# Two graph layers on one core: 0/1 matrices turned by bf16 products, a PSUM bank for the nodes alone, and a later first row-by-row tile

## The chip, the core and the metric

The kernel runs on one core of a Trainium2 chip. The metric is device time in microseconds: 3799.89 us, the median of three runs (3799.22 to 3804.44). One further execution was profiled; the views quoted below come from it.

A core has five engines, each working through its own instructions in order: PE (TensorE: matrix products, written to PSUM), DVE (VectorE), ACT (ScalarE), POOL (GpSimd; here it issues almost only indirect DMAs, which gather rows of a table by an index column) and SP (SyncE; here it issues plain DMAs). They wait for each other by semaphores. PSUM holds 8 banks of 128 partitions by 512 float32.

## The reference

Two message-passing layers over 6250 nodes and 200000 edges, which are sorted by their target `dst`, each behind a layer norm and a relu:

```
h = relu(layernorm(x))
z = h @ W                                   # 8 heads of 16
el, er = z.attn_l, z.attn_r                 # per head
e = leaky_relu(el[src] + er[dst], 0.2)
a = exp(e - segment_max(e, dst)[dst])
x = x + segment_sum(z[src] * a, dst) / segment_sum(a, dst) + bias
h = relu(layernorm(x))
s, v = h parts @ W_up                       # 32 scalars, 32 vectors of 3
w = silu(silu(edge_attr_8 @ A1 + b1) @ A2 + b2) @ A3
m = segment_sum(products of s[src], v[src], edge_attr_4 and w, dst) / 10
x = x + m @ W_out
```

## The kernel before

**Tiles and blocks.** The edges are cut into 1563 tiles of 128, the tiles into 98 blocks of `KB` = 16 (the last has 11 tiles). For a tile the kernel needs the 128 rows of a node table that `src` names: table `t0` (136 floats a row: z and el) in the first layer, `t1` (128 floats) in the second. They come to a buffer `z` of a block in four ways:

- `gather` (L839): one indirect DMA on POOL for one tile. It is the usual way: 2972 of them in all.
- `rows_by_row` (L1142): for the last tile of each block in the list `by_row` (L1109), SP issues 128 plain DMAs, one per row, into a tile `r`; `filled` (L1167) has ACT copy it into `z`. `rows_by_row` is a generator that hands back after 4 DMAs, and `rows_until(rows, block)` (L1162) draws from it until a count that follows the block number. `by_row` is 3, 6, ..., 93 in both layers.
- Dense blocks (first layer: 21 to 93 where not in `by_row`): tile 14 of the block is computed on PE as a product of 0/1 matrices with the whole table, which lies in SBUF in three bf16 parts (`t0s`). `asked(k)` (L1255) loads three tiles of the table into `zr` by SP, `split(k)` (L1270) has DVE cut them into the parts.
- The rows of the first block and of 7 tiles of block 1 (`KX = KB + 7`, L806) are gathered from `x` itself before `t0` exists, and `v["rows_of"]` (L1129) computes z and el for them on the spot.

There are five buffers for `z` besides `z_first`, used in turn. The gathers of block g+5 overwrite those of block g, and each waits for the product that last read its tile.

**The loop of the first layer.** After a prologue (layer norm and `t0` for all nodes, the check that the edges are sorted evenly), one turn g of a loop (L1570) works on several blocks at once: `logits(c)` and `maxima(c)` for block g, the attention weights and `sums` of block g-1, and `masks_of`, `turned`, `er_of` and `er_sum` for block g+1. The order of PE, DVE, ACT and SP is the written order; POOL's is too, since gathers alone stand on it. The first turns place this on SP: `rows_until(rows, g + 0.5)`, node outputs, `asked(g - 2)`, `node_rows`, `rows_until(rows, g + 1)`; and `split(g - 3)` at the end of the turn on DVE.

- `one_hot` (L1174): DVE compares `iota_p` with the local target of each edge; the result `s` is a 0/1 matrix of 128 edges by 128 nodes in float32, four tiles at a time. It is the stationary operand of `sums` (L1420).
- `turned` (L1332): PE transposes `s`, a float32 transpose per tile, into bank `p_d`; ACT copies it to bf16 `d` (L1339). `er_of` (L1341) multiplies `d` by the node values er, and `er_sum` (L1352) adds the three bf16 parts.
- `masks_of` (L1323): one product into bank `p_m` and a copy to `mk`, 385 columns: 128 for same target as the edge before, a separating column that is always -1e30, 128 for same target as the first edge of the next tile, 128 for the last of the tile before.
- `node_x` to `node_out` (L1436 to L1491): in every second turn, two blocks have completed 64 nodes each; the new x, its layer norm and the rows of `t1` are computed: `node_t` transposes into `p_n` (L1467), ACT makes `h_t` (L1469), `node_s` multiplies by W_up into `p_n` (L1474), ACT writes `sv` (L1479), and SP stores it to `t1` and to `t1z`, a copy of `t1` whose last three tiles are zero.

The bank `p_n` (L1247) is shared: the node products, `iota_p` (read by each `one_hot`) and `er_p` (written by each `er_sum`, read by the next `logits`) lie in it.

**Between the layers.** The last turn is g = 95; the blocks behind it follow in straight code (L1661 on). The first 24 gathers of the second layer (`early`, L1667) read `t1z`, which is complete when the last node tile but three is stored; the gathers after them read `t1` and wait for its last store. The second layer starts the same way, with `rows_by_row` for `t1` and its own unit loop (`tensor_weights`, `messages`, `sums1`).

Of the kernel before, what the change touches and what calls it, by code (L numbers as in the profile page):

```python
# [741 lines left out]
def tile_even_edges(  # L742
# [31 lines left out]
    TG = -(-TU // P)  # L774
    NB = -(-TU // KB)
    KT = [min(KB, TU - b * KB) for b in range(NB)]
    MC = 3 * P + 1
    assert NB % 2 == 0 and NB > 4 and KT[-1] > 3 and NX == NB // 2 + 1
    dram = ctx.enter_context(tc.tile_pool(name="fdram", bufs=1, space=DRAM))
    keep = ctx.enter_context(tc.tile_pool(name="keep", bufs=1))  # L780
# [22 lines left out]
    src_col = keep.tile([P, TU], I32, name="fsrc")  # L803
    z_first = keep.tile([P, KB, ZW], F32, name="fz_first")
    ok_i = keep.tile([1, 1], I32, name="fok")
    KX = KB + 7  # L806
    z_second = keep.tile([P, KB, ZW], F32, name="fz_second")
    other = keep.tile([P, KB, ZW], F32, name="fz_other")
    flat = other.rearrange("p k f -> p (k f)")
# [201 lines left out]
def even_edges(tc, v):  # L1011
# [8 lines left out]
    with ExitStack() as ctx:  # L1020
# [41 lines left out]
        with tc.tile_pool(name="fbuild", bufs=1) as build:  # L1062
# [21 lines left out]
            nc.vector.memset(eq[:, :, P : P + 1], 0.0)  # L1084
            nc.vector.tensor_tensor(eq[:, :, :P], e_i, q_i, OP.is_equal)
            nc.vector.memset(eq[:, :, 0:1], 0.0)
            nc.vector.tensor_tensor(eq[:, :, P + 1 : 2 * P + 1], e_i,
                                    nxt_i.to_broadcast([P, TG, P]), OP.is_equal)
            nc.vector.tensor_tensor(eq[:, :, 2 * P + 1 :], e_i,
                                    q_i[:, :, 0:1].to_broadcast([P, TG, P]), OP.is_equal)  # L1090
            for g in range(TG):
                nc.scalar.activation(masks[:, g, :], eq[:, g, :], AF.Copy, bias=-BIG, scale=BIG)
# [13 lines left out]

            by_row = [b for b in range(3, NB - 2) if b % 3 == 0]  # L1109
            at = [const.tile([P, P], I32, name=f"fat{i}") for i in range(2)]  # L1110
            with tc.tile_pool(name="fat_ps", bufs=1, space=PSUM) as at_ps, \
                    tc.tile_pool(name="fat_c", bufs=1) as at_c:
# [29 lines left out]
        def rows_by_row(layer, table, width):  # L1142

            flat = table.rearrange("r f -> (r f)").bitcast(mybir.dt.uint8)
            size = 4 * width
            for b in by_row:
                to = row_pool.tile([P, width], F32, name="r")
                rows_by_row.tiles[layer, b] = to
                for e in range(P):
                    if e % 32 == 0:  # L1150
                        _, offs = nc.values_load_multi_w_load_instructions(
                            at[layer][b : b + 1, e : e + 32], engines=[mybir.EngineType.SP],
                            min_val=0, max_val=(NX * P - W0 - 1) * size,
                            skip_runtime_bounds_check_because="a row of the table")
                    nc.sync.dma_start(to[e : e + 1, :].bitcast(mybir.dt.uint8),
                                      flat[ds(offs[e % 32], size)].unsqueeze(0))
                    if e % 4 == 3:
                        yield
# [2 lines left out]

        def rows_until(rows, block):  # L1162

            while rows_until.n < (block + 3) * P / 12 and next(rows, 0) is None:
                rows_until.n += 1

        def filled(layer, b, z, width):  # L1167
            if b in by_row:
                nc.scalar.copy(z[:, KB - 1, :width], rows_by_row.tiles.pop((layer, b)))

        def one_hot(t, m, iota, pool=s_pool):
# [29 lines left out]
        dense = {b for b in range(-(-NX // TS) + 4, NB - 4) if b not in by_row}  # L1201
        dense1 = set(range(10, NB - 4, 4))

        ranges = []
# [34 lines left out]
        with tc.manual_schedule(engines=in_order), \  # L1239
# [83 lines left out]
            def masks_of(c):  # L1323
                o, kr = c["o"], c["kt"] * H
                g, j = divmod(c["b"], P // KB)
                p_m = l0_ps.tile([P, 512], F32, name="p_m")
                nc.tensor.matmul(p_m[:kr, :MC], rsel[:, j, o * H : o * H + kr], masks[:, g, :],  # L1327
                                 start=True, stop=True)
                mk = c["mk"] = l0.tile([P, MC], F32, name="mk", bufs=4)
                nc.scalar.copy(mk[:kr], p_m[:kr, :MC])  # L1330

            def turned(c, q):  # L1332
                if 4 * q < c["kt"]:
                    m = min(4, c["kt"] - 4 * q)
                    p_d = l0_ps.tile([P, 4, P], F32, name="p_d")
                    for k in range(m):
                        nc.tensor.transpose(p_d[:, k, :], c["s"][q][:, k, :], ident)  # L1337
                    d = c["d", q] = l0.tile([P, 4, P], BF, name="d", bufs=4)
                    nc.scalar.copy(d[:, :m], p_d[:, :m])  # L1339

            def er_of(c, q):  # L1341
                if 4 * q < c["kt"]:
                    b = c["b"]
                    er_w = (er3o if b % 2 else er3)[:, b // 2, :, :].rearrange("p s h -> p (s h)")
                    if q == 0:
                        c["p_er"] = l0_ps.tile([P, KB, 3, H], F32, name="p_er")
                    for k in range(min(4, c["kt"] - 4 * q)):
                        nc.tensor.matmul(c["p_er"][:, 4 * q + k].rearrange("p s h -> p (s h)"),
                                         c["d", q][:, k, :], er_w, start=True, stop=True)

            def er_sum(c, aside=False):
                kt = c["kt"]  # L1352
                er = c["er"] = l0.tile([P, KB, H], F32, name="er") if aside else er_p
                nc.vector.tensor_reduce(er[:, :kt], c["p_er"][:, :kt].rearrange("p t s h -> p t h s"),
                                        AX.X, OP.add)

            def logits(c, bank="pe"):
# [9 lines left out]
            def maxima(c):  # L1367

                kr, mk, pe = c["kt"] * H, c["mk"], c["pe"]
                m0, m1 = pe[:kr, P : 2 * P], pe[:kr, 3 * P :]  # L1370
                nc.vector.tensor_tensor_scan(m0, mk[:kr, :P], pe[:kr, :P], 0.0, OP.add, OP.max)
                nc.vector.tensor_tensor_scan(m1[:, ::-1], mk[:kr, P:0:-1], m0[:, ::-1], 0.0,
                                             OP.add, OP.max)
                mx = c["mx"] = l0.tile([P, 2], F32, name="mx", bufs=4)
                nc.scalar.copy(mx[:kr], m1[:, :: P - 1])
# [18 lines left out]
            def weights(c):  # L1394

                kr, pe, mk, ud = c["kt"] * H, c["pe"], c["mk"], c["ud"]
                m1, m2 = pe[:kr, 3 * P :], pe[:kr, P : 2 * P]
                nc.vector.scalar_tensor_tensor(m2, mk[:kr, P + 1 : 2 * P + 1], ud[:kr, 0:1],
                                               m1, op0=OP.add, op1=OP.max)
                a = l0.tile([P, P], F32, name="a")  # L1400
                nc.vector.scalar_tensor_tensor(a[:kr], mk[:kr, 2 * P + 1 :], ud[:kr, 1:2],
                                               m2, op0=OP.add, op1=OP.max)
                nc.vector.tensor_sub(a[:kr], pe[:kr, :P], a[:kr])
                nc.scalar.activation(a[:kr], a[:kr], AF.Exp)
# [111 lines left out]
            def take_rows(g):  # L1516
                if g == 1:
                    cs[1]["z"] = gather(buffer(), t0, range(KX, 2 * KB), ZW, KX - KB)
                elif 0 < g < NG:
                    c = cs[g]  # L1520
                    t = c["b"] * KB + c["o"]
                    c["z"] = gathered(t0, [k for k in range(t, t + c["kt"])
                                           if not (c["b"] in by_row and k % KB == KB - 1)
                                           and not (c["b"] in dense and k % KB == KD)], ZW)

            def bank_of(c, bank="p_u"):
                if c["o"] == 0:
                    bank_of.now = l0_ps.tile([P, 512], F32, name=bank)
                c["p_u"] = bank_of.now

            def ended(c, st):
# [161 lines left out]
            neighbours(c1, c2, None)  # L1693
            weighted(c3, 0)
            sums(c4, 8)
            bank_of(c3, "p_m")
            sums(c3, 0)
            weights(c2)
            weights(c1)
# [28 lines left out]
        with tc.manual_schedule(engines=in_order), \  # L1728
# [209 lines left out]
            def take_rows(b):  # L1938
# [2 lines left out]
                                         max(NE - b * KB, 0))  # L1941
                elif b < NB:
                    blk[b]["z"] = gathered(t1, [k for k in range(b * KB, b * KB + KT[b])
                                                if not (b in by_row and k % KB == KB - 1)
                                                and not (b in dense1 and k % KB == KD)], P)

            rows, rows_until.n, late, x_of = rows_by_row(1, t1, P), 0, [], {}
# [13 lines left out]
            for i, u in enumerate(us):  # L1961
# [196 lines left out]
```

## Time and profile before

| | |
|---|---|
| time, median of three runs | 3799.89 us |
| time of the profiled execution | 3804.17 us |
| span of the profiled execution | 3802.3 us |
| mean granted TensorE clock | 0.915 of full speed |
| PE busy | 3119.3 us (82%) |
| DVE busy | 2560.8 us (67%) |
| ACT busy | 1412.3 us (37%) |
| POOL busy | 2836.8 us (75%), 3005 instructions |
| gathers on POOL (L839) | 944 ns each |
| row DMAs on SP | 3968 in each layer |

The first layer's loop lies at about 82 to 1896 us, the second layer from about 1929 us on. A busy share is an average: an engine that issues DMAs spends time between two of them that isn't counted as busy. A line of the timeline gives the start, the duration, the engine, the source line, the operation with its tiles and shapes, and how many instructions follow each other; in brackets stands how long the engine had been idle before and what ended that. A line of the waits gives the waiting instruction, what it waited for, the sum in us, how often, and the longest.

### The profile page before, as it was taken

What the parts mean: (1) busy time and instruction counts of PE and PEld (TensorE: products, weight loads), DVE (VectorE), ACT (ScalarE), POOL (GpSimd) and SP (SyncE); (2) the same over time, 40 slices, a digit from 0 to 9 for tenths busy, and PEclk for the clock granted to TensorE, in tenths of its full rate; (3) what the DMA queues carried; (4) which work ended last, traced back from release to release, by engine and by line L of the source; (5) the groups of instructions that cost most, each with busy time, mean ns of one, the idle gap of its engine ahead of it and who ended that gap; (6) DMA issues with size and microseconds to landing.
All of it is one profiled execution on the core that took longest, in us unless ns stands there. A gap on an engine that the chain in (4) does not pass through costs nothing. (4 is left out here: it accounts for less than half of the span.)

```text
span 3802.3 us, 72404 instructions
## 1 busy us (share of the span) xinstructions
PE 3119.3 (82%) x18514; PEld 2471.7 (65%) x18514; DVE 2560.8 (67%) x6137; ACT 1412.3 (37%) x3637; POOL 2836.8 (75%) x3005
## 2 busy tenths in 40 slices
PE   5466687888887787787787898999999899999997
PEld 4466566666666666666666677677677677777775
DVE  7366666666666656666556777777777777777776
ACT  4233333333333333333324444444444444444443
POOL 7677777777777777777677777777777777777776
PEclk7666698988998998999789999999999999999999
DMA  6233323322222223222223222222222222222222
GB/s 163 56 78 78 78 67 68 69 68 68 68 68 70 68 68 68 68 68 69 60 68 93 75 64 63 64 63 64 64 64 63 64 64 63 64 64 64 64 68 52
DMA packets 213547, 264.35 MB, mean 70 GB/s; under 512 B 77936, under 2 KB 164560, under 8 KB 213120
## 3 DMA queue, kind: packets, MB, share of 16 engines
q0 software_dynamic: 95840, 202.46, 22.5%
q1 hardware_dynamic: 116848, 57.10, 5.5%
q8 instruction: 148, 2.42, 0.3%
q14 instruction: 279, 2.29, 0.2%
q10 hardware_dynamic: 432, 0.09, 0.0%
HBM read 237.94 MB, written 21.14 MB: 68 GB/s over the span
## 5 line engine op out<-in xcount | busy, mean ns | idle before, releaser
L839 POOL DMA_INDIRECT fz<-ft,fsrc x1764 | 1665.9, 944 | 558.4 <-issue 323.8
L1817 PE MATMUL p_u<-mj,s 128*128 128x256 f32 x3126 | 761.6, 387 | 87.6 <-DVE mj L1809 86.6
L1817 PEld LDWEIGHTS p_u<-mj,s 128*128 128x128 f32 x3126 | 579.5, 191 | 214.7 <-DVE mj L1809 139.4
L839 POOL DMA_INDIRECT fz_other<-ft,fsrc x594 | 561.0, 944 | 181.2 <-issue 106.7
L839 POOL DMA_INDIRECT fz_second<-ft,fsrc x590 | 559.7, 949 | 182.8 <-issue 108.3
L1784 ACT ACTIVATE p_w<-p_w,yb 128x64 f32<-128x64 f32 x1563 | 450.4, 288 | 117.1 <-PE p_w L1780 73.3
L1306 PE MATMUL p_x<-t0s,fz_first 128*128 128x408 bf16 (+1 forms) x2448 | 483.5, 348 | 0.0
L1780 PE MATMUL p_w<-fa3p,h 128*128 128x256 f32 x1564 | 406.3, 383 | 0.0
L1780 PEld LDWEIGHTS p_w<-fa3p,h 128*128 128x128 f32 x1564 | 285.7, 193 | 114.9 <-issue 48.6
L1337 PE MATMUL p_d<-fident,s 128*128 128x128 f32 x1563 | 297.1, 322 | 72.3 <-ACT d L1339 70.7
L1765 ACT ACTIVATE h<-p_h,fb 128x512 f32<-128x512 f32 x196 | 134.7, 687 | 588.9 <-PE p_h L1763 582.0
L1306 PEld LDWEIGHTS <-fz_first 128*128 128x128 bf16 x2448 | 241.2, 101 | 156.3 <-issue 18.0
L1420 PE MATMUL p_u<-fz,s 128*128 128x136 f32 x1846 | 285.9, 319 | 10.1 <-DVE fz L1415 10.1
L1339 ACT CAST d<-p_d 128x512 bf16<-128x512 f32 x391 | 228.7, 585 | 176.2 <-PE p_d L1337 92.5
L1337 PEld LDWEIGHTS p_d<-fident,s 128*128 128x128 f32 x1563 | 213.6, 168 | 108.0 <-ACT d L1339 100.3
L1420 PEld LDWEIGHTS p_u<-fz,s 128*128 128x128 f32 x1846 | 271.6, 226 | 12.5 <-DVE fz L1415 11.4
L1174 DVE TENSOR_TENSOR s<-p_n,fdloc 128x512 f32<-128x512 f32 x391 | 266.7, 684 | 8.5 <-ACT sv L1479 3.1
L1174 DVE TENSOR_TENSOR s<-p_i,fdloc 128x512 f32<-128x512 f32 x391 | 266.1, 680 | 3.8 <-ACT p_i L1759 3.8
L1763 PE MATMUL p_h<-ft,fa1p 128*128 128x128 f32 x1568 | 214.8, 281 | 61.9 <-DMA ft<-in_e_f_dram 61.8
L1763 PEld LDWEIGHTS p_h<-ft,fa1p 128*128 128x128 f32 x1568 | 207.4, 196 | 85.5 <-issue 64.2
L1330 ACT COPY mk<-p_m 128x385 f32<-128x385 f32 (+1 forms) x99 | 47.6, 481 | 563.9 <-PE p_m L1327 560.5
L1770 ACT ACTIVATE h<-p_h,fb 128x512 f32<-128x512 f32 x196 | 134.7, 687 | 259.5 <-PE p_h L1767 259.4
(284 smaller groups left out, 4762.9 us busy)
## 6 DMA issues: line engine op xcount, KB each, us to landing
r<-ft SPq DMA_DIRECT2D x3968, 0.5 KB
r<-ft SPq DMA_DIRECT2D x3968, 0.5 KB
fz<-ft,fsrc POOLq DMA_INDIRECT x1764
fz_other<-ft,fsrc POOLq DMA_INDIRECT x594
fz_second<-ft,fsrc POOLq DMA_INDIRECT x590
fx<-x SPq DMA_DIRECT2D x47, 160.0 KB
ft<-in_e_f_dram SPq DMA_DIRECT2D x98, 64.0 KB
t1s<-fx SPq DMA_DIRECT2D x7, 576.0 KB
```

The source lines that it names most:

```text
L839: nc.gpsimd.indirect_dma_start(out=to[:, k, :width], out_offset=None, in_=table, in_offset=bass.IndirectOffsetOnAxis(ap=src_col[:, t : t + ...
L1174: nc.vector.tensor_tensor(s[:, :m], iota[:, None, :].to_broadcast([P, m, P]), dloc[:, t : t + m].unsqueeze(2).to_broadcast([P, m, P]), OP. ...
L1306: nc.tensor.matmul(c["p_x"][:, :m, :], c["oh", k // half][:, k % half, :], t0s[:, i::NR, s, :], start=k == 0 and s == 0, stop=k == NR - 1 ...
L1337: nc.tensor.transpose(p_d[:, k, :], c["s"][q][:, k, :], ident)
L1339: nc.scalar.copy(d[:, :m], p_d[:, :m])
L1420: nc.tensor.matmul(c["p_u"][:, :ZW], c["s"][k // 4][:, k % 4, :], c["z"][:, k, :], start=c["o"] + k == 0, stop=c["o"] + k == KT[c["b"]] - 1)
L1763: nc.tensor.matmul(p_h[:, q, :], a1p[:, q0 + q, :], c["ft"], start=True, stop=True)
L1765: nc.scalar.activation(c["h1"], p_h, AF.Silu, bias=b1)
L1770: nc.scalar.activation(h2, p_h, AF.Silu, bias=b2)
L1780: nc.tensor.matmul(w[:, k : k + n].rearrange("p k a u -> p (k a u)"), c["h2"][q // 4][:, q % 4, :], a3p[:, :n].rearrange("p k f -> p (k f) ...
L1784: nc.scalar.activation(w[:, k, ::2, :], w[:, k, ::2, :], AF.Copy, scale=c["yb"][:, k0 + k, 0:1])
L1817: nc.tensor.matmul(blk[b]["p_u"][:, :MW], u["s"][:, k, :], u["mj"][:, k, :], start=k0 + k == 0, stop=k0 + k == KT[b] - 1)
```

## The change

- `KX` is `KB + 9`: nine tiles of block 1, not seven, are gathered from `x` in the prologue and computed on the spot.
- `by_row` is a list for each layer: 6, 9, ..., 93 in the first (30 tiles), 3, 6, ..., 93 as before in the second (31). Tile 15 of block 3 is gathered by POOL in the first layer. `rows_until` no longer adds three blocks to its count; the call of the second layer adds them itself. So in the first layer the same count of DMAs is reached three blocks later.
- `p_n` belongs to the nodes alone (and to one late block's logits). `iota_p` moves to the fourth quarter of `p_m`, `er_p` to the fourth quarter of `p_er`; both banks are now allocated once instead of in each turn.
- The masks have 384 columns. The separating column stands in four fixed `mk` tiles of 3 by 129 columns, set once.
- `turned` multiplies the upper bf16 halves of the float32 `s` (a 0 or a 1 has nothing in the lower half) by a bf16 identity, where it transposed `s` in float32.

```
-    MC = 3 * P + 1
+    MC = 3 * P
-    KX = KB + 7
+    KX = KB + 9
...
-            by_row = [b for b in range(3, NB - 2) if b % 3 == 0]
+            by_row = [list(range(6 - 3 * i, NB - 2, 3)) for i in range(2)]
...
-                gz += [(k, min(4, KX - k)) for k in range(KB, KX, 4)]
+                gz += [(k, min(5, KX - k)) for k in range(KB, KX, 5)]
...
-            for b in by_row:
+            for b in by_row[layer]:
...
-            while rows_until.n < (block + 3) * P / 12 and next(rows, 0) is None:
+            while rows_until.n < block * P / 12 and next(rows, 0) is None:
...
-            p_n = l0_ps.tile([P, 512], F32, name="p_n")
-            er_p, iota_p = p_n[:, P : 2 * P].rearrange("p (t h) -> p t h", h=H), p_n[:, 3 * P :]
+            p_n, p_m, p_er = (l0_ps.tile([P, 512], F32, name=n) for n in ("p_n", "p_m", "p_er"))
+            iota_p = p_m[:, 3 * P :]
+            er_3 = p_er[:, : 3 * P].rearrange("p (t s h) -> p t s h", s=3, h=H)
+            er_p = p_er[:, 3 * P :].rearrange("p (t h) -> p t h", h=H)
             nc.scalar.copy(iota_p, iota)
+            mks = [l0c.tile([P, 3, P + 1], F32, name=f"mk{i}") for i in range(4)]
+            for mk in mks:
+                nc.vector.memset(mk[:, :, P:], -BIG)
+            identb = l0c.tile([P, P], BF, name="fidentb")
+            nc.vector.tensor_copy(identb, ident)
...
-                p_m = l0_ps.tile([P, 512], F32, name="p_m")
-                mk = c["mk"] = l0.tile([P, MC], F32, name="mk", bufs=4)
-                nc.scalar.copy(mk[:kr], p_m[:kr, :MC])
+                mk = c["mk"] = mks[0]
+                mks.append(mks.pop(0))
+                nc.scalar.copy(mk[:kr, :, :P], p_m[:kr, :MC].rearrange("p (a e) -> p a e", e=P))
...
+                    halves = c["s"][q].bitcast(BF).rearrange("p k (n a) -> p k n a", a=2)
                     for k in range(m):
-                        nc.tensor.transpose(p_d[:, k, :], c["s"][q][:, k, :], ident)
+                        nc.tensor.matmul(p_d[:, k, :], halves[:, k, :, 1], identb, start=True, stop=True)
...
-                rows_until(rows, b + (k0 + 4) / KB)
+                rows_until(rows, b + (k0 + 4) / KB + 3)
```

More of the change, by code (lines that the diff above doesn't have):

```diff
@@ L1083, in even_edges @@
             eq = build.tile([P, TG, MC], F32, name="feq")
-            nc.vector.memset(eq[:, :, P : P + 1], 0.0)
             nc.vector.tensor_tensor(eq[:, :, :P], e_i, q_i, OP.is_equal)
             nc.vector.memset(eq[:, :, 0:1], 0.0)
-            nc.vector.tensor_tensor(eq[:, :, P + 1 : 2 * P + 1], e_i,
+            nc.vector.tensor_tensor(eq[:, :, P : 2 * P], e_i,
                                     nxt_i.to_broadcast([P, TG, P]), OP.is_equal)
-            nc.vector.tensor_tensor(eq[:, :, 2 * P + 1 :], e_i,
+            nc.vector.tensor_tensor(eq[:, :, 2 * P :], e_i,
                                     q_i[:, :, 0:1].to_broadcast([P, TG, P]), OP.is_equal)
@@ L1162, in rows_until @@
         def rows_until(rows, block):
-            while rows_until.n < (block + 3) * P / 12 and next(rows, 0) is None:
+            while rows_until.n < block * P / 12 and next(rows, 0) is None:
                 rows_until.n += 1
         def filled(layer, b, z, width):
-            if b in by_row:
+            if b in by_row[layer]:
                 nc.scalar.copy(z[:, KB - 1, :width], rows_by_row.tiles.pop((layer, b)))
@@ L1200, in even_edges @@
         TS = 3
-        dense = {b for b in range(-(-NX // TS) + 4, NB - 4) if b not in by_row}
+        dense = {b for b in range(-(-NX // TS) + 4, NB - 4) if b not in by_row[0]}
         dense1 = set(range(10, NB - 4, 4))
@@ L1344, in er_of @@
                     er_w = (er3o if b % 2 else er3)[:, b // 2, :, :].rearrange("p s h -> p (s h)")
-                    if q == 0:
-                        c["p_er"] = l0_ps.tile([P, KB, 3, H], F32, name="p_er")
                     for k in range(min(4, c["kt"] - 4 * q)):
-                        nc.tensor.matmul(c["p_er"][:, 4 * q + k].rearrange("p s h -> p (s h)"),
+                        nc.tensor.matmul(er_3[:, 4 * q + k].rearrange("p s h -> p (s h)"),
                                          c["d", q][:, k, :], er_w, start=True, stop=True)
@@ L1353, in er_sum @@
                 er = c["er"] = l0.tile([P, KB, H], F32, name="er") if aside else er_p
-                nc.vector.tensor_reduce(er[:, :kt], c["p_er"][:, :kt].rearrange("p t s h -> p t h s"),
+                nc.vector.tensor_reduce(er[:, :kt], er_3[:, :kt].rearrange("p t s h -> p t h s"),
                                         AX.X, OP.add)
@@ L1370, in maxima @@
                 m0, m1 = pe[:kr, P : 2 * P], pe[:kr, 3 * P :]
-                nc.vector.tensor_tensor_scan(m0, mk[:kr, :P], pe[:kr, :P], 0.0, OP.add, OP.max)
-                nc.vector.tensor_tensor_scan(m1[:, ::-1], mk[:kr, P:0:-1], m0[:, ::-1], 0.0,
+                nc.vector.tensor_tensor_scan(m0, mk[:kr, 0, :P], pe[:kr, :P], 0.0, OP.add, OP.max)
+                nc.vector.tensor_tensor_scan(m1[:, ::-1], mk[:kr, 0, P:0:-1], m0[:, ::-1], 0.0,
                                              OP.add, OP.max)
@@ L1397, in weights @@
                 m1, m2 = pe[:kr, 3 * P :], pe[:kr, P : 2 * P]
-                nc.vector.scalar_tensor_tensor(m2, mk[:kr, P + 1 : 2 * P + 1], ud[:kr, 0:1],
+                nc.vector.scalar_tensor_tensor(m2, mk[:kr, 1, :P], ud[:kr, 0:1],
                                                m1, op0=OP.add, op1=OP.max)
                 a = l0.tile([P, P], F32, name="a")
-                nc.vector.scalar_tensor_tensor(a[:kr], mk[:kr, 2 * P + 1 :], ud[:kr, 1:2],
+                nc.vector.scalar_tensor_tensor(a[:kr], mk[:kr, 2, :P], ud[:kr, 1:2],
                                                m2, op0=OP.add, op1=OP.max)
@@ L1522, in take_rows, with bank_of @@
                     c["z"] = gathered(t0, [k for k in range(t, t + c["kt"])
-                                           if not (c["b"] in by_row and k % KB == KB - 1)
+                                           if not (c["b"] in by_row[0] and k % KB == KB - 1)
                                            and not (c["b"] in dense and k % KB == KD)], ZW)
-            def bank_of(c, bank="p_u"):
+            def bank_of(c, bank=None):
                 if c["o"] == 0:
-                    bank_of.now = l0_ps.tile([P, 512], F32, name=bank)
+                    bank_of.now = l0_ps.tile([P, 512], F32, name="p_u") if bank is None else bank
                 c["p_u"] = bank_of.now
@@ L1695, in even_edges @@
             sums(c4, 8)
-            bank_of(c3, "p_m")
+            bank_of(c3, p_m)
             sums(c3, 0)
@@ L1943, in take_rows @@
                     blk[b]["z"] = gathered(t1, [k for k in range(b * KB, b * KB + KT[b])
-                                                if not (b in by_row and k % KB == KB - 1)
+                                                if not (b in by_row[1] and k % KB == KB - 1)
                                                 and not (b in dense1 and k % KB == KD)], P)
```

## The prediction

> **What bounds the kernel now.** I read the table by stage first, since the shares of the whole span (PE 82%, POOL 75%) do not tell which engine never rests.
>
> ```profile
> core 0: us, PE busy (x) PEld busy (x) DVE busy (x) ACT busy (x) POOL busy (x), PEclk, DMA share, GB/s
> 150.00:200.00 50.00, 18.13 (x98) 16.63 (x99) 20.61 (x65) 7.52 (x18) 27.79 (x30) 0.53 0.24 53
> 500.00:1000.00 500.00, 402.64 (x2969) 314.77 (x2969) 313.05 (x667) 159.04 (x357) 378.03 (x401) 0.90 0.30 69
> 3000.00:3500.00 500.00, 455.36 (x2259) 352.94 (x2259) 381.68 (x946) 220.95 (x621) 377.81 (x401) 1.00 0.25 63
> ```
>
> The reader is to see 401 POOL instructions in 500 us in both layers: one gather every 1.247 us, though the layers load PE quite differently. Between 150 and 200 us there are only 30. So next come POOL's waits:
>
> ```profile
> POOL fz L839 <- issue: 324.2, 1063, 0.3
> POOL fz L839 <- PE p_u L1420: 69.0, 182, 13.7
> POOL fz_first L839 <- DMA ft1z<-sv: 11.4, 1, 11.4
> POOL fz L839 <- PE p_h L1861: 7.6, 2, 7.3
> POOL fz_second L839 <- DMA ft<-zt: 3.2, 1, 3.2
> ```
>
> Nearly every gather follows 0.30 us after the one before. Four pauses alone are longer: 3.2 us before the first gather of `t0`, 13.7 us in the first layer, 11.4 and 7.3 us between the layers. POOL is therefore the bound from 41 us to its last gather at 3787 us, and the time changes by gathers added or taken (1.25 us each) and by these four pauses; other engines count only through them.
>
> The timeline around the 13.7 us pause, SP, ACT, DVE and POOL in turn:
>
> ```profile
> 74.51 58.45 SPq L1155 DMA_DIRECT2D r<-ft  x152
> 133.01 0.37 SPq L1430 DMA_DIRECT2D x<-in_e_xp_dram  x1
> 133.48 34.28 SPq L1155 DMA_DIRECT2D r<-ft  x84
> 167.82 0.33 SPq L1263 DMA_DIRECT2D zr<-ft  x1
> ...
> 124.68 0.30 ACT L1169 COPY fz<-r 128x136 f32<-128x136 f32 x1 [7.46 <-DMA r<-ft]
> ...
> 170.62 0.58 DVE L1229 CAST t0s<-zr 128x408 bf16<-128x408 f32 x1 [31.09 <-DMA zr<-ft]
> ...
> 185.37 0.94 POOL L839 DMA_INDIRECT fz<-ft,fsrc  x1 [13.65 <-PE p_u L1420]
> ```
>
> SP issues 236 row DMAs (0.385 us each) before it comes to the first load of `zr`, at 167.8 us. DVE, with its written order, stands 31.09 us before that `split`; `sums` of block 3 comes late, and the gathers of block 8 wait for block 3's buffer.
>
> Two waits tell of the bank `p_n`, and two lines of PE in turn 63 price a transpose:
>
> ```profile
> DVE p_n L1354 <- ACT h_t L1469: 104.8, 46, 4.7
> PE p_n L1474 <- DVE s L1174: 80.3, 45, 1.8
> ...
> 1291.66 0.63 PE L1337 MATMUL p_d<-fident,s 128*128 128x128 f32 x4
> 1292.13 0.25 PE L1348 MATMUL p_er<-fer,d 128*128 128x24 bf16 x4
> ```
>
> In every second turn `er_sum` waits for the nodes' `h_t`, and `node_s` waits for a `one_hot`, only because they touch one bank. Yet `logits` of blocks 21 to 92 starts 30 to 40 us after its rows were gathered, with 18.7 us a turn against POOL's 15 x 1.247 = 18.7: compute trails POOL and runs level with it.
>
> **The change, part by part.** The sum is made against the profiled execution, 3804.17 us: its span of 3802.3 and 1.87 around it. The median is 4.3 us lower; I take the difference over to it.
>
> *First row tile at block 6, pace three blocks later.* Before the first `zr` SP now issues 108 row DMAs (27 steps of 4 by turn 2), not 236: 128 x 0.385 = 49.3 us earlier, so near 118.5 us, landed 2.4 us later. DVE comes to that `split` at 139.5 us now, and some 6 us earlier without the 6.1 us for which `logits` of block 3 waits on its row tile (within ACT's 7.46): near 133. The 31.09 us wait goes, with 12 us to spare. What is late next: SP needs some 18 us a turn (`zr` starts at 186.1, 203.3, 223.5, 242.0 us), so `split` may wait again for a microsecond or three in turns 4 to 19, as it does now (45.8 us over the 14 later waits). That pace still beats POOL's 16, 16 and 15 gathers, 19.5 us a block. `sums` of block 3 ends near 152 us, and block 8's gather is due at 171.7: the pause falls to the usual 0.30. Gain 13.65 - 0.30 = 13.35 us. The gather of block 3's last tile comes onto POOL: +1.25.
>
> *Nine rows of x.* Two gathers move from behind the wait for `t0` (3.18 us) to in front of it. At best they fill that pause and save 2 x 1.25 = 2.5. At worst the pause is spent and beside DVE's comparisons they stretch (1.78 and 1.99 us instead of 0.94 stand at 42.26 and 44.34), and nothing is saved. I take 1.25, in the middle: the first of the two falls before those comparisons, the second beside them. That pays for block 3's gather; together between -1.25 and +1.25. Computing two more tiles delays turn 0 by 1 to 2 us of DVE and PE work (0.42 us of moments, 0.29 of normalizing a tile, a transpose and a product); the z of blocks 1 and 2 lies there 30 us before it is used, which covers it.
>
> *Nodes' bank.* It takes 80.3 / 45 = 1.8 us from PE's path in every second turn, and up to 2.3 from DVE's. `iota_p` in `p_m` adds a wait: the masks product waits for the first `one_hot` of a turn, the second `one_hot` for ACT's copy of the masks. Product and copy are 0.33 + 0.48 us; the two scans between the `one_hot`s take 0.86. Behind the product stand the transposes, behind the `one_hot` the neighbours' sums. At worst it costs 0.5 us in turns where PE waits for DVE; often nothing, because the `one_hot` ended long before (at 1282.8, with the product at 1288.2).
>
> *bf16 products.* No row shows one. The nearest are the four L1348 products of the same width of weights, 0.25 us with 24 columns; the farthest, the float32 transposes, 0.63 (no gain). 104 more columns at 0.43 ns (nine products of 408 columns end 1.72 us after the first starts) are 45 ns each, which makes some 0.4: 0.23 less for four, 0.9 a turn. A price above 0.63 is open too, if reading every second half is slow; it is a rival below. The 385th column, the fixed `mk` and five settings outside the loop cost nothing on POOL's path.
>
> One rule speaks against this part: the Trainium skill, "Perfetto Trace Analysis", section "Transposes", wants a logical transpose done as a transpose, not as an ordinary product. By it the 0.9 us would be zero or a loss; no run here shows it yet, and the sum below stays what it is by either, since it needs no faster turn.
>
> *Between the layers.* Both pauses are compute's trail. `logits` of block 95 starts at 1873.8 us, 24.5 us after its rows (1849.2), and the last gather of the layer ends at 1883.2. The store of `t1z` follows 20.8 us behind that `logits`, so its pause needs a trail of at most 24.5 - 11.1 = 13.4. `t1` is stored 35.6 us after `logits` of block 96, whose rows are there 14.0 us before POOL ends; POOL has 24 early gathers (29.9 us) to do; so its pause needs a trail of at most 8.6. In turn 4 the trail was 59.9 us, 37 of them from the two waits that go: about 22 remain. Turns 5 to 20 (18.7 us against 19.5) take off 13 as they do now, and the four turns from 92 to 95 took off 13 as well: the trail is at its floor of some 2 us even if turns get no shorter, and sooner with 0.9 + 0.9 us off each. Gain 11.42 - 0.30 and 7.28 - 0.30: 11.12 + 6.98 = 18.1 us.
>
> The second layer keeps its place behind POOL (its compute starts 2.7 us before POOL's 25th gather now, about 5 after), and the end (last gather, its landing, last sums, output, 15 us) stays. Sum: 13.35 + 18.1 = 31.4 us; 3804.2 - 31.4 = 3772.8 for a profiled execution, 3768.5 for the median.
>
> The clock: after idle stretches PE's records are half as fast (a granted 0.50 while it waited after 172 us, and 0.67 to 0.72 from 200 to 500 us). A compute that waits for rows will idle more. The skill's "TensorE: Matmul & The Clock Gate" (section "Why this matters for your kernels") says the same, with a limit near 3 us of idle. The rows bound it: at 0.7 the turns of 200 to 460 us took 18.7, under the 19.5 that POOL needed there.
>
> **The rivals.**
>
> 1. *The boundary keeps its pauses* (14%). If `zr` or the row tiles still hold the turns, or something in the epilogue not in my reading does, the trail stays above 13.4 us. For it: turns of 18.7 against 18.7 catch up nothing in blocks 21 to 92. Against it: the start alone removes 37 us of trail. It would be 3799.9 - 13.35 = 3786.5.
> 2. *Nothing moves* (6%). Block 3's sums are late for another reason, such as SP standing before `zr`, whose buffer DVE clears at 106 us; or every pause returns elsewhere. Against it: 12 us of room. About 3800, and within 0.2%.
> 3. *Compute becomes the bound: slower* (5%). Place: `turned` and the masks in all 96 turns. If four half-word products took 1.12 us, as float32 ones do at half clock (1327.2 to 1330), a turn would grow by 2.0, less the 0.9 of the bank. 75 dense turns of 19.8 against POOL's 18.7 are 83 us, less some 20 that five buffers absorb: 3799.9 - 13.35 + 63 = 3849. It decides from 19.3 us a turn on: 0.55 x 75 - 20 outweighs 13.35 and the 0.2%. Against it: 1.1 us more a turn than any row shows.
>
> **How the numbers follow.** My forecast has 75%. Its own range is 3763 to 3775: the x rows and block 3 (1.25 either way), a `t0` wait filled wholly, up to 5 us of the second boundary pause kept (its room is the smallest), and the 4 us between executions. To leave out no more than two in ten, the range takes in most of rival 1: 3762 to 3787. 0.2% (7.6 us) is about what a measurement can tell from no change. Faster by more: the forecast, rival 1 and a little of rival 2, 0.90; same 0.05; slower 0.05.
>
> **What would show it.** POOL's waits over 0.4 us: only the one for `t0`, no 13.7, 11.4 or 7.3. DVE's first wait for `zr` under 5 us; the two waits on `p_n` gone from the lists; at least 38 gathers in every 50 us from 100 us on. Four turned tiles in 0.3 to 0.45 us at full clock. `logits` waiting for gathers in the dense turns, with a trail of 2 to 5 us at block 95. It would be wrong if the trail at block 95 is above 13 us, if gathers of the first layer wait for `sums` in many turns, or if a gather no longer takes 1.247 us.

## The result, and the profile after

The changed kernel takes 3773.81 us (median of four runs, 3773.4 to 3774.0) against 3801.62 us of the kernel before (four runs, 3799.22 to 3804.44): a ratio of 0.9926, 95% interval 0.9909 to 0.9944. That is 27.8 us less. Run again later, the pair gave 3772.89 and 3799.88 us, ratio 0.9935 (0.9918 to 0.9951). The prediction was 3768.5 us, range 3762 to 3787. Between the two profiled executions, where the prediction made its sum, the step is 3804.17 to 3773.64 us, and the span went from 3802.3 to 3771.6.

The table by stage after the change; the columns are as in the table before:

```profile
core 0: us, PE busy (x) PEld busy (x) DVE busy (x) ACT busy (x) POOL busy (x), PEclk, DMA share, GB/s
150.00:200.00 50.00, 31.82 (x242) 28.95 (x243) 37.03 (x88) 21.13 (x49) 37.81 (x41) 0.73 0.34 81
500.00:1000.00 500.00, 388.58 (x2985) 298.46 (x2983) 306.97 (x662) 155.26 (x356) 377.94 (x401) 0.88 0.30 68
3000.00:3500.00 500.00, 458.23 (x2277) 354.30 (x2276) 377.85 (x936) 218.26 (x613) 377.99 (x401) 1.00 0.25 64
```

POOL still issues 401 gathers in 500 us in both layers: the gather itself costs what it did. Between 150 and 200 us it issues 41, where it issued 30. Some of POOL's waits, the longest among them:

```profile
POOL fz_second L839 <- issue: 108.5, 353, 1.1
POOL fz L839 <- PE p_u L1427: 56.4, 185, 0.3
...
POOL fz_first L905 <- DVE stx L819: 2.7, 1, 2.7
```

The last number of a line is the longest single wait. But for the first of them, every gather of `t0`, `t1z` and `t1` now follows 0.3 us after the one before; ahead of that first one 1.1 us is left of the 3.2 (the 2.7 us is in the prologue, ahead of the gathers of x, and was there before). The pauses of 13.7, 11.4 and 7.3 us are gone. What stands in their place, in the timelines of SP, DVE and POOL:

```profile
55.07 7.75 SPq L1154 DMA_DIRECT2D r<-ft  x24
62.87 0.37 SPq L1437 DMA_DIRECT2D x<-in_e_xp_dram  x1
63.34 34.17 SPq L1154 DMA_DIRECT2D r<-ft  x84
97.60 0.33 SPq L1270 DMA_DIRECT2D zr<-ft  x1
...
128.96 0.57 DVE L1228 CAST t0s<-zr 128x408 bf16<-128x408 f32 x1
...
1838.73 0.29 DVE L1369 TENSOR_TENSOR e_s<-fz_other,p_er 128x128 f32<-128x128 f32 x1 [8.55 <-DMA fz_other<-ft,fsrc]
...
171.75 0.94 POOL L839 DMA_INDIRECT fz<-ft,fsrc  x1 [0.30 <-PE p_u L1427]
...
1870.96 0.94 POOL L839 DMA_INDIRECT fz_first<-ft1z,fsrc  x1 [0.30 <-issue]
```

SP has 108 row DMAs before the first `zr`, which it loads at 97.6 us and not at 167.8. DVE comes to the `split` at 128.96 us and doesn't wait. The gather of block 8 stands at 171.75 us, 0.30 after its predecessor. At block 95, `logits` (L1369) waits 8.55 us for its rows, where it came 24.5 us after them. The first gather of the second layer (1870.96 us) follows 0.30 us after the last one of the first, like any other. Compute now waits for POOL, and the lists of waits say so:

```profile
DVE e_s L1369 <- DMA fz<-ft,fsrc: 185.8, 41, 8.2
DVE e_s L1369 <- DMA fz_other<-ft,fsrc: 80.4, 17, 8.6
DVE e_s L1369 <- DMA fz_second<-ft,fsrc: 65.4, 15, 7.0
...
DVE s L1173 <- ACT mk L1337: 2.6, 7, 1.3
...
PE p_m L1333 <- DVE s L1173: 3.7, 14, 0.3
```

In place of the waits on the shared bank, `logits` waits for gathers in most turns. The two waits that the change adds (the masks product for the first `one_hot`, the second `one_hot` for the copy of the masks) take 6.3 us over both engines and the whole first layer.

### The profile page after: what moved, and what is told of

It is laid out like the page before. It is cut to its first block, busy times and chain, and to the rows that moved or that the text cites. A ratio compares the mean times of both kernels' runs of the same rounds, so it can differ in the third digit from the quotient of the medians.

```text
span 3771.6 us, 72078 instructions
## 1 busy us (share of the span) xinstructions
PE 3054.4 (81%) x18520; PEld 2399.1 (64%) x18520; DVE 2548.8 (68%) x6147; ACT 1406.9 (37%) x3638; POOL 2839.5 (75%) x3006
## 5 line engine op out<-in xcount | busy, mean ns | idle before, releaser
L1337 ACT COPY mk<-p_m 128x384 f32<-128x384 f32 (+1 forms) x99 | 47.5, 480 | 684.1 <-PE p_m L1333 684.1
L1173 DVE TENSOR_TENSOR s<-p_m,fdloc 128x512 f32<-128x512 f32 x391 | 266.2, 683 | 3.9 <-ACT mk L1337 2.6
L1770 PE MATMUL p_h<-ft,fa1p 128*128 128x128 f32 x1568 | 214.6, 281 | 59.9 <-DMA ft<-in_e_f_dram 59.9
L1346 PE MATMUL p_d<-fidentb,s 128*128 128x128 bf16 x1563 | 184.0, 253 | 72.0 <-ACT d L1348 69.9
L1811 DVE TENSOR_REDUCE vd<-vy 128x128 f32<-128x384 f32 x391 | 229.8, 588 | 0.0
```

Of the source, the lines that this page charges most:

```text
L1173: nc.vector.tensor_tensor(s[:, :m], iota[:, None, :].to_broadcast([P, m, P]), dloc[:, t : t + m].unsqueeze(2).to_broadcast([P, m, P]), OP. ...
L1346: nc.tensor.matmul(p_d[:, k, :], halves[:, k, :, 1], identb, start=True, stop=True)
L1770: nc.tensor.matmul(p_h[:, q, :], a1p[:, q0 + q, :], c["ft"], start=True, stop=True)
L1811: nc.vector.tensor_reduce(vd, vy.rearrange("p t i u -> p t u i"), AX.X, OP.add)
```

## The experiments

In the table below "trail" is the time from the last gather of a block to the start of its `logits`, as in the prediction; the turn is the mean from block 22 to block 40. "Pauses" are the waits of POOL at the start of the first layer's loop, for `t1z` and for `t1`, in this order ("none": all three are the usual 0.3; the wait for `t0` isn't among them). All rows are from profiled executions.

| kernel | first `zr` on SP | trail at block 4 | turn | trail at block 95 | pauses | us of that execution |
|---|---|---|---|---|---|---|
| before | 167.8 | 59.9 | 18.83 | 24.5 | 13.7, 11.4, 7.3 | 3804.17 |
| before, once more | 167.1 | 57.3 | 18.76 | 20.0 | 11.0, 7.1, 8.1 | 3798.65 |
| rows_only | 116.5 | 24.9 | 18.79 | 1.7 | none | 3781.33 |
| bf16_only | 167.9 | 59.8 | 18.27 | 1.7 | 11.7 | 3783.91 |
| bank_only | 148.6 | 39.2 | 18.28 | 1.7 | none | 3781.32 |
| no_rows | 147.8 | 42.2 | 17.77 | 1.7 | none | 3777.68 |
| f32_turned | 97.6 | 28.7 | 18.77 | 1.8 | none | 3771.75 |
| after | 97.6 | 18.5 | 18.76 | 1.8 | none | 3773.64 |
| after, once more | 97.6 | 18.7 | 18.68 | 1.8 | none | 3771.91 |
| all_dense | 98.1 | 18.8 | 18.65 | 1.7 | none | 3743.51 |

The turns of rows_only, f32_turned, both rows of after and all_dense start from a trail of 2 to 4 us there; except in all_dense, whose trail grows, they are POOL's turns and not compute's own.

### The row part alone

```
-            by_row = [b for b in range(3, NB - 2) if b % 3 == 0]
+            by_row = [list(range(6 - 3 * i, NB - 2, 3)) for i in range(2)]
...
-            while rows_until.n < (block + 3) * P / 12 and next(rows, 0) is None:
+            while rows_until.n < block * P / 12 and next(rows, 0) is None:
...
-                rows_until(rows, b + (k0 + 4) / KB)
+                rows_until(rows, b + (k0 + 4) / KB + 3)
```

> The kernel before with the later first row tile and the later pace of the first layer alone. The forecast's reading (all pauses are the trail that the first turns leave): SP reaches the first load of zr near 118 us instead of 167.8, the pause of 13.7 us is gone, one gather more (+1.25), and because 37 us of trail are missing, the two pauses between the layers go too, although no turn gets shorter: 3799.9 - 13.35 + 1.25 - 18.1 = 3769.7 us. Rival (the boundary needs shorter turns): only the first pause goes, pauses of 11.4 and 7.3 us stay: 3787.8 us. Rival (sums of block 3 are late for another reason): 3801.

It took 3782.92 us (median of four), 0.9948 (0.9931 to 0.9965) of before, whose runs on this chip have a median of 3802.71. All three pauses are gone, so the last two go although no operation got cheaper: from block 22 on the turn is 18.79 us, as before, and the trail at block 4 is 35 us lower. One thing comes on top: from block 4 to block 22 a turn takes 18.46 us on average, where it took 18.92. What is gone there are most waits of `split` for its later loads of `zr`: 45.8 us behind the first of 31.1, now 3.2 in all. DVE's waits for `zr`, in the kernel before and here:

```profile
DVE t0s L1229 <- DMA zr<-ft: 76.9, 15, 31.1
...
DVE t0s L1229 <- DMA zr<-ft: 3.2, 2, 2.6
```

At block 22 the trail is 4.0 us, and it stays under 8 us up to block 92. SP loads the first `zr` at 116.5 us, where 118 was expected. The mechanism is the forecast's; the time is 13 us above it. Some 8 of these lie in a place that no theory named: in this profile a gather of the second layer comes every 1.2511 us, not 1.2485, on each of 2973 gathers. (Another 4 are those between the profiled execution of before and its median, which the expectation took over: counted from 3804.17 us the same sum is 3774.0, with the longer step 3781.7, and the profiled execution took 3781.33.) POOL's waits show no pause: the longest of a gather of `t0` or `t1` is the one for `t0` itself, and those for `sums` are the usual 0.3 us:

```profile
POOL fz L839 <- PE p_u L1420: 56.2, 184, 0.3
...
POOL fz_second L839 <- DMA ft<-zt: 3.1, 1, 3.1
```

### The bf16 products alone

```
-                        nc.tensor.transpose(p_d[:, k, :], c["s"][q][:, k, :], ident)
+                        nc.tensor.matmul(p_d[:, k, :], halves[:, k, :, 1], identb, start=True, stop=True)
```

> The kernel before with the bf16 products of turned alone. The forecast's reading: the pause of 13.7 us at the start stays (SP's order is untouched); with 1.1 us of PE less in each dense turn the trail of 30 to 40 us shrinks over some 75 turns to its floor of about 2 us, so the pauses of 11.4 and 7.3 us go: 3799.9 - 18.1 = 3781.8 us. Rival (a turn isn't set by PE's transposes, the trail stays): 3799.9 us with all pauses.

The profiled execution took 3783.91 us; the other seven 3791.1 to 3793.2. Over all, 0.9973 (0.9962 to 0.9984) of before. In the profile the boundary pauses are gone and the one at the start is left:

```profile
183.86 0.94 POOL L839 DMA_INDIRECT fz<-ft,fsrc  x1 [11.73 <-PE p_u L1423]
```

The turn is 18.27 us, 0.5 shorter than before, and the trail falls from 34.7 us at block 22 to 3.5 at block 82. So the rival (that PE's transposes don't set the turn) falls. The profiled execution is 2 us from the expected 3781.8, the median 10. The profile has a gather every 1.2486 us; with 1.2512, as in the other three profiles of this chip, it would be about 7.7 us longer, near 3792. That this is what the other seven did is an inference: they have no trace, and a pause between the layers that came back in them would also explain their times.

### The nodes' bank alone

```
+            p_n, p_m, p_er = (l0_ps.tile([P, 512], F32, name=n) for n in ("p_n", "p_m", "p_er"))
+            iota_p = p_m[:, 3 * P :]
...
+            er_p = p_er[:, 3 * P :].rearrange("p (t h) -> p t h", h=H)
...
-                mk = c["mk"] = l0.tile([P, MC], F32, name="mk", bufs=4)
+                mk = c["mk"] = mks[0]
```

> The kernel before with the nodes' own bank alone (iota_p in p_m, er_p in p_er, fixed mk, 384 columns; float32 transposes, 23 x tiles, first row tile at block 3). The forecast's reading: the waits of er_sum for h_t and of node_s for one_hot go, some 0.9 us a turn; the trail shrinks to its floor before block 95 and both boundary pauses go; the 13.7 us at the start stays if SP's row DMAs begin at 74.5 us as before: 3781.8 us; it goes too (3768.5) if they begin near 55 us as they do in the changed kernel. Rival (the waits moved on to another engine, turns as long as before): 3799.9.

3780.03 us, 0.994 (0.9923 to 0.9957) of before. All three pauses are gone, the one at the start too: the second branch, where SP's row DMAs begin near 55 us, is what happened. What SP waited for between 45 and 80 us, in the kernel before and here:

```profile
SPq L1430 <- DVE fh L960: 16.7, 1, 16.7
SPq L1430 <- PE p_z L983: 4.6, 1, 4.6
```

```profile
SPq L1434 <- ACT fmasks L1091: 1.5, 1, 1.5
...
SPq L1434 <- DVE fdloc L1103: 0.6, 1, 0.6
```

L1430 and L1434 are the same line: the load of a node tile of `x`, which stands ahead of the row DMAs on SP. Before, it waits 21.3 us for the normalizing and the products of the prologue, with which it shares no data; here for 2.1 us, and for others. The likely reason is shared memory: the part moves `mk` to another pool, and the tiles behind it get other places. (That is argued from the list of waits; neither the places of the tiles nor which of the moved ones does it was tried.) The turn is 18.28 us, 0.5 shorter than before. The gathers' step is 1.2513 us here too, which is some 8 us of the distance to the expected 3768.5.

### The change without the row part

```
-            by_row = [list(range(6 - 3 * i, NB - 2, 3)) for i in range(2)]
+            by_row = [b for b in range(3, NB - 2) if b % 3 == 0]
...
-            while rows_until.n < block * P / 12 and next(rows, 0) is None:
+            while rows_until.n < (block + 3) * P / 12 and next(rows, 0) is None:
```

> The changed kernel without the later row tile and pace: first row tile at block 3 and three blocks ahead again, all else as changed. If SP's later reach of zr is all that makes the start pause, 128 row DMAs more put the first zr load near 97.6 + 49.3 = 147 us; DVE then waits some 20 us before that split, sums of block 3 end near 163 us, before the gather of block 8 is due at 171.8: no pause, one gather fewer, 3773.8 - 1.25 = 3772.6 us. Rival (the row part alone removes the start pause): 13.4 us of pause come back, 3786; and with the longer trail one or both boundary pauses as well, up to 3804.

3778.02 us, 0.9937 (0.992 to 0.9953) of before, and no pause. SP has 236 row DMAs again ahead of `zr`, DVE waits 23.4 us before that `split` (20 expected), and the gather of block 8 still comes 0.30 us after its predecessor: SP's head start of 20 us is enough. The rival falls. The expected 3772.6 are missed by 5.4 us, with a step of 1.2513 us. The free turn is 17.77 us: both parts together take 1.0 us off it, the sum of what each does alone.

### Both kernels once more, and float32 transposes in the changed kernel

The first two are the kernels as they stand. The third, against the changed kernel:

```
-                        nc.tensor.matmul(p_d[:, k, :], halves[:, k, :, 1], identb, start=True, stop=True)
+                        nc.tensor.transpose(p_d[:, k, :], c["s"][q][:, k, :], ident)
```

> The changed kernel once more, as a control beside the others on one chip. In its first profile a gather came every 1.2477 us; in the profiles of rows_only, bank_only and no_rows every 1.2503 us, 0.0026 us more on each of some 2970 gathers, 7 us in all. If the step belongs to the execution or the chip: 3773.8 to 3781 us, whatever step its profile shows explaining the difference. If the step belongs to the built kernel: 1.2477 and 3773.8 us again.

> The kernel before once more, as a control. If the step of the gathers belongs to the execution or the chip, its profile may show 1.2503 us; then POOL's pauses between the layers are shorter by some 3 us (compute trails less behind a slower POOL) and the time is within 5 us of 3802. If it belongs to the built kernel: 1.2477 us, pauses of 13.7, 11.4 and 7.3 us.

> The changed kernel with the float32 transposes in turned again: later row tile, nodes' bank and 25 x tiles kept. The forecast's reading: no pause comes back, since the trail needs no shorter turn; turns that run free take 0.5 us longer, the time is that of the changed kernel beside it within 2 us. Rival (the bf16 products carry the gain between the layers): pauses of 11.4 and 7.3 us, 18 us more.

The changed kernel took 3772.89 us (3771.91 to 3776.07) and its step is 1.2487 us again, on another chip than rows_only, bank_only and no_rows. The kernel before has 1.2486. Since bf16_only had 1.2486 among three of 1.2511 to 1.2513, the step is not the chip's alone. That one execution of bf16_only lies 7 to 9 us below the other seven of the same build would fit a step that belongs to the execution, but no kernel was profiled at both steps. That stays open.

The kernel before once more has shorter pauses, at the same step:

```profile
POOL fz L839 <- PE p_u L1420: 67.4, 186, 11.0
...
POOL fz L839 <- PE p_h L1861: 8.4, 2, 8.1
POOL fz_first L839 <- DMA ft1z<-sv: 7.1, 1, 7.1
```

The three make 26.2 us where the first profile has 32.4: 6.2 us less, and the execution is 5.5 us shorter (3798.65 to 3804.17). So in these two executions of the kernel before the time differs about as its pauses do.

With float32 transposes the changed kernel takes 3771.75 us (one execution), as long as with bf16 products, and has no pause. The bf16 products carry nothing of this change's gain once the other parts are in.

### A dense tile in the blocks that have a row tile

```
-        dense = {b for b in range(-(-NX // TS) + 4, NB - 4) if b not in by_row[0]}
+        dense = set(range(-(-NX // TS) + 4, NB - 4))
```

> The changed kernel with tile 14 of the blocks with a row tile computed from the table too: 25 more dense blocks (21, 24, ..., 93), so 25 gathers fewer. The forecast's reading (POOL is the bound, compute waits some 4.5 us a turn for rows, and a dense tile costs a turn some 5 us of PE and DVE in a third of the turns): compute keeps up, 25 x 1.2475 = 31 us less than the changed kernel beside it, 3742 to 3750. Rival (compute becomes the bound in the first layer: turns of over 18.3 us against POOL's 44/3 x 1.2475 = 18.3): the trail grows and gathers wait for sums, nothing to 15 us is gained.

3744.18 us (3741.62 to 3745.79), 0.9856 (0.984 to 0.9873) of before and 28.7 us below the changed kernel beside it: it beats both. No gather of `t0` or `t1` waits over 1.1 us, so nearly the whole 31 us arrive. Yet the rival is half right. A row of the table by stage of this kernel:

```profile
500.00:1000.00 500.00, 441.40 (x3445) 323.17 (x3443) 339.49 (x709) 156.01 (x357) 378.25 (x400) 0.96 0.30 68
```

PE is busy 88% of the time (78% in the changed kernel), the turn is 18.65 us against POOL's 44/3 gathers, 18.3, and the trail grows from 1.8 us at block 22 to 24.2 at block 82. Five buffers hold that, and the turns from block 92 on, where the dense tiles end, bring the trail back to 1.7 at block 95. In these blocks compute is now the slower of the two, so a further step of this kind in them has no room.

### The x rows, the form of the turning, and one step further

bf16_again is bf16_only unchanged.

> The kernel of bf16_only once more. In its profiled execution a gather came every 1.2486 us in the second layer and it took 3783.9 us; its other seven executions took 3791 to 3793. If the gathers' step belongs to the execution and not to the kernel (1.2512 us in the profiles of rows_only, bank_only and no_rows, on the same chip), it takes about 3782 to 3785 us here if the changed kernel's profiled step of 1.2488 holds here, and up to 3793 with the longer step. Rival (the kernel itself has two courses, such as one boundary pause that comes and goes): its profile shows a pause of 7 to 11 us between the layers beside a time near 3792.

x_7, against the changed kernel:

```
-    KX = KB + 9
+    KX = KB + 7
```

> The changed kernel with 23 tiles of x rows as before (KX = KB + 7). The forecast's reading: the wait for t0 before the first gather is back at 3.2 us, and the gathers of block 2 begin 1.25 us later (0 to 2.5): the time of the changed kernel + 1.25. From the two profiles it should be 1.6 (54.68 against 53.08 us for the first gather of block 2).

turn_bf16, against the changed kernel:

```
-                    p_d = l0_ps.tile([P, 4, P], F32, name="p_d")
+                    p_d = l0_ps.tile([P, 4, P], BF, name="p_d")
...
-                        nc.tensor.matmul(p_d[:, k, :], halves[:, k, :, 1], identb, start=True, stop=True)
+                        nc.tensor.transpose(p_d[:, k, :], halves[:, k, :, 1], identb)
```

> The changed kernel with transposes of the bf16 halves (into a bf16 p_d) in the place of bf16 products with the identity. If a transpose is the better form: four tiles in less than the 0.38 us of the four products, or ACT's copy of a bf16 tile in less than 0.587 us. Rival (for PE both are one pass of 128 bf16 columns): 0.38 us and 0.587 us again. POOL is the bound either way: the time of the changed kernel within 2 us.

denser, against all_dense:

```
-        dense1 = set(range(10, NB - 4, 4))
+        dense1 = set(range(10, NB - 4, 3))
```

> all_dense, and in the second layer a dense block in every third block (10, 13, ..., 91: 28) and not in every fourth (21): 7 gathers fewer. If compute has room in the second layer too (PE is busy 92% of it), 7 x 1.248 = 8.7 us less than all_dense's 3744.2: 3735.5. Rival (a dense block's products fill PE): gathers of the second layer wait for sums, 3744 or more.

The chip of these four ran everything much longer: the kernel before took 6094.37 us there (median of seven), bf16_again 6034.24, x_7 5958.8, turn_bf16 5987.06, denser 5955.37 us (5926.51 to 5976.84); x_7 and turn_bf16 ran once each. Against before beside it bf16_again is 0.9907 (0.9872 to 0.9943) and denser 0.9772 (0.9724 to 0.9819). Instructions last as long as elsewhere (the copy of `d` 587 ns), but between them ACT stands still for up to 32 us and DVE for up to 46 us without a releaser in this core's records. The two largest sums among ACT's waits in x_7:

```profile
ACT mk L1337 <- remote: 1053.0, 60, 24.8
ACT h L1772 <- remote: 361.2, 38, 28.1
```

What held them wasn't found. Compute is the bound there (in x_7 the gathers into `fz` alone wait 664 us for `sums`), so the four times say nothing on POOL's path: the expected times of all four, and with them the questions of bf16_again, x_7 and denser, are without a verdict. The price of an operation can still be read, since both forms ran on that chip. ACT's copies and PE's products in a part of the first layer, of x_7 (bf16 products), then of turn_bf16 (bf16 transposes):

```profile
L1348 ACT CAST d<-p_d 128x512 bf16<-128x512 f32 x172 | 100.9, 587 | 115.7 <-remote 70.7 <-PE p_er L1355 20.9 <-PE p_d L1346 13.1
L1346 PE MATMUL p_d<-fidentb,s 128*128 128x128 bf16 x684 | 83.5, 261 | 31.9 <-ACT d L1348 31.5 <-issue 0.5
```

```profile
L1348 ACT COPY d<-p_d 128x512 bf16<-128x512 bf16 x171 | 100.3, 587 | 97.4 <-remote 59.7 <-PE p_er L1355 19.9 <-PE p_d L1346 14.5
L1346 PE MATMUL p_d<-fidentb,s 128*128 128x128 bf16 x684 | 84.2, 262 | 31.3 <-ACT d L1348 31.3
```

The second number behind the bar is the mean of one in ns: 261 and 262 for PE, 587 and 587 for ACT. Nor does a mix of clocks hide a difference: in both runs four in a row take 0.38 or 0.39 us at full clock and 0.59 at the lower one. A transpose of bf16 is not cheaper than a product with the identity, and the copy doesn't gain from bf16 either.

The x rows can be read from the profiles of the other runs, at the first gather of block 2 (the tenth gather of `t0` with 23 tiles of x, the eighth with 25). With 23 tiles of x it starts at 54.68, 56.38, 54.55, 54.88 and 55.90 us (both profiles of before, rows_only, bf16_only, bank_only), with 25 at 53.08, 52.46, 52.60, 52.62 and 52.04 (both of after, no_rows, all_dense, f32_turned): means of 55.3 and 52.6, 2.7 us apart. (The four kernels beside before and after differ from these in other parts too; none of them touches what lies ahead of this gather on POOL.)

## Why the prediction was right

**The bound.** POOL was the bound and still is: the gather kept its 1.248 us, and all that moved are pauses and the number of gathers. Each stretch of 50 us between 50 and 500 us holds 40 or 41 of its instructions.

**The start pause** (13.35 us forecast). It went, 13.65 to 0.30 us. Of the chain, the row DMAs are as forecast (rows_only: first `zr` at 116.5 us against 118.5), but in the changed kernel it is at 97.6, because SP's row DMAs begin at 55 us and not at 74.5. The prediction didn't see this, and it is enough by itself (bank_only, no_rows). So the size of the term is right, but the cause that the prediction gives is one of two, either of which suffices; of the second it knew nothing. `sums` of block 3 starts at 140.9 us (184.3 before); the forecast had its end near 152.

**Between the layers** (18.1 us forecast). Both pauses went, 11.42 and 7.28 to 0.30 each. The reading that a smaller trail at the start is enough holds: rows_only has before's turn from block 22 on and no pause. It was even safer than forecast, which counted on 13 us taken off in turns 5 to 20 and on `split` waiting for `zr` as before: rows_only takes off 21 between block 4 and block 22 (24.9 to 4.0), with 3.2 us of such waits and not 45.8. The trail at block 95 was forecast at some 2 us and is 1.8; in turn 4 it was forecast at 22 and is 18.5. The limit of 13.4 us for the `t1z` pause was borne out by a second case: in the repeat of before the trail is 20.0 us, which makes a pause of 6.6 above the usual step, and 6.8 is measured.

**Shorter turns** (0.9 us a turn for each of the two parts, not needed by the sum). Each takes 0.5, both 1.0. The PE prices were right: four bf16 products take 0.38 us where four float32 transposes took 0.63, as the forecast's 0.4.

```profile
1294.23 0.38 PE L1346 MATMUL p_d<-fidentb,s 128*128 128x128 bf16 x4
```

Of the 1.0 us a turn that this frees on PE, half lay beside other work. The Trainium skill's "Perfetto Trace Analysis", section "Transposes", wants a transpose done as a transpose and not as a product. The measurement shows 262 ns for a transpose and 261 for a product in bf16, so neither form costs or saves against the other here. What saves here is the type, not the form.

**The x rows and block 3's gather** (-1.25 and +1.25). The gather is there. The x rows gave 1.6 us in the pair of first profiles and 2.7 in the mean of five against five: the better end of the bound, 2.5, was nearer than the middle (1.25), and the mean even lies beyond it. Two profiles of the kernel before differ by 1.7 us there, so the mean is the better reading, 1.6 is the pair's own, and 0.2 beyond the bound is within the scatter.

**The sum** was 31.4 us. The measured terms of the first pair are 13.35 + 11.12 + 6.98 + 1.60 - 1.25 = 31.8; the span fell by 30.7. Of the 1.1 us between, some 1.2 lie from 200 to 460 us, where seven gathers take 1.11 to 1.28 us instead of 0.94 (two before). The forecast for a profiled execution, 3772.8 us, is 0.8 from the measured 3773.64.

**The median** was forecast 5.3 us too low. The step that failed is that the 4.3 us between the profiled execution and the median were taken over. The changed kernel's four runs lie within 0.6 us, and its profiled one is 0.17 from their median; without that term the forecast is 1 us off. Two things are seen in its place. With its fourth run the median of the kernel before is 3801.62 us, so the profiled execution lies 2.6 us above it and not 4.3. And of two profiled executions of that kernel, 5.5 us apart, the longer has 6.2 us more of pauses (before_again), which a kernel without pauses can't have. That pauses explain all of the scatter isn't shown: run again, the changed kernel spread from 3771.91 to 3776.07 us, without a trace of the longest.

**The rivals.** That the boundary keeps its pauses fell with the result, as did that nothing moves; rows_only adds that the boundary needs no cheaper turn. Compute as the bound was priced by a half-word read of 1.12 us for four tiles; they take 0.38 (0.59 at the lower clock). Its mechanism showed only where more work was put in, in all_dense. The clock fell as the forecast said it would, with more idle time (0.88 in the table by stage where it was 0.90), and cost nothing, since compute waits for rows.

## What to carry to other kernels

A wait of the bounding engine is worth its own length and no more, and several edits that each remove it do not add up: here the later row tiles alone or the bank alone (with the tiles that it moves) remove all three pauses, and the bf16 products two of them (in the one execution of theirs with a trace). To price an edit off the bound, follow how far the other engines trail it, and what trail the next hard boundary allows. Once no pause is left, only fewer operations of the bounding engine bring more, until the room that the edits made is used up (25 gathers fewer gave 28.7 us, and the trail grew by 22).

## What was unexpected of the hardware

- The step of POOL's gathers in the second layer is not one number: 1.2485 to 1.2488 us in seven profiles, 1.2511 to 1.2513 in three (rows_only, bank_only, no_rows), with the same instructions there. The difference lies in the gather itself (944 ns, and 946 in the three), not in the 0.3 us between two. On 2970 gathers that is 7 to 8 us, a quarter of what the change brought, and it comes unannounced: a run must be judged by its own step. What sets it is open.
- A load that uses no data of the prologue waited 21 us for it, and waits 2 us in the kernel that moves quite other tiles (`mk` among them). That its tile took the memory of prologue tiles is the likely reason and isn't shown.
- On one chip all kernels, the one before among them, took some 1.6 times as long, with instructions of the usual duration and stalls of up to 46 us between them. What held ACT and DVE there is open.
